# Grouped-query attention of a fused four-layer kernel: value and output weights folded into one product, heads summed in one PSUM bank, and the stage written out as a fixed order of pairs

## The chip, the cores and the metric

The kernel runs on one core of one Trainium2 chip. A core has TensorE (PE, with its weight loads listed apart as PEld), VectorE (DVE), ScalarE (ACT), GpSimd (POOL) and SyncE (SP, which here only issues transfers). The metric is the device time of one execution in microseconds (us). Before the change the median of three runs is 2576.98 us, from 2571.02 to 2581.21.

## The reference, cut to what matters

Four layers run one after another on `x` of shape (4, 512, 128): a gated scan, a mixture of eight experts, grouped-query attention, and six layers of windowed attention with a feed-forward. After each layer the input is added and a layer normalisation follows. The change lies in the third, with `NH, NKV, D = 8, 4, 128` and T = 512 positions a row:

```
q = (x @ Wq).reshape(b, t, NH, D).transpose(0, 2, 1, 3)
k = (x @ Wk).reshape(b, t, NKV, D).transpose(0, 2, 1, 3)
v = (x @ Wv).reshape(b, t, NKV, D).transpose(0, 2, 1, 3)
q = q * cos + rotate_half(q) * sin
k = k * cos + rotate_half(k) * sin
k, v = repeat(k, 2, axis=1), repeat(v, 2, axis=1)
attn = einsum('bhtd,bhsd->bhts', q, k) / sqrt(D)
attn = softmax(where(causal, -inf, attn))
out  = einsum('bhts,bhsd->bhtd', attn, v)
return out.transpose(0, 2, 1, 3).reshape(b, t, NH * D) @ Wo
```

Two query heads share one key and value head. The output is linear in `v` and in `Wo`, so `(attn @ v_kv) @ Wo_h` equals `attn @ (x @ (Wv_kv @ Wo_h))`, and the sum over the heads can be taken in any order.

## The kernel before, in words

Everything is float32 but the masks, which are bfloat16 and reach the scores through a product with a bfloat16 identity (`ident_h`). The 512 positions of a row are four chunks of 128. PSUM has eight banks of 512 float32 columns: the tags "mm" and "tr" have two one-bank buffers each that are used in turn, and "S" and "o" have one buffer of two banks each. The batch rows are `xB[b]` on entry to the third layer and `xA[b]` on leaving it.

The stage runs over 32 steps, one for each row b and query head h, and lets three pieces of work overlap by lag: at step i it projects head i, does the softmax of head i-1 and weighs the values of head i-2.

- `project`: with the first head of a row it transposes the row (`x2T`) and makes the values of all four key heads (L362, copied out to `V`). For each key head, and for each query head, `rotated` makes one 512-column product (L340), three products with the cosine and sine tables on DVE (L344, L346) and one sum on POOL (L350).
- `softmax`: for each of the four chunks of queries, of 128, 256, 384 and 512 keys, a mask product of the whole width (L387) and the score product (L390) add up in one bank of "S" or "o". DVE takes the maximum (L393) and scales it (L394), ACT takes the exponential and its sum (L397). When all four are done DVE takes the reciprocal (L401) and divides the four chunks (L404).
- `weigh`: ten 128 x 128 transposes (L419) in four groups, four copies to `gpT` (L423), four products of `V` with them that add up in one bank (L426), and a copy to `oT`. After the last head of a row, 32 products with `Wo` (L436) sum the heads, DVE adds the row (L441), and the layer normalisation follows.

The copies out of PSUM go through `evac`, which gives two of three to ACT (L86) and the third to DVE (L88), by a running count. Beyond the loops' lag, the order of the instructions on each engine is left to the tile framework's scheduler. The fourth layer, further on, is handled otherwise: its steps are a list written by hand (`TURN`), and manual dependencies keep every engine to that order.

Two things about the surroundings are used below. The stage's buffers take memory that the expert stage frees when its last row is normalised. The fourth layer starts when the last row of `xA` has been normalised, transposed and copied to `sA`; its first product is L550.

Of the kernel before, what the change touches and what calls it, by code (L numbers as in the profile page):

```python
# [8 lines left out]
F32 = mybir.dt.float32  # L9
BF16 = mybir.dt.bfloat16  # L10
AF = mybir.ActivationFunctionType
ALU = mybir.AluOpType
AX = mybir.AxisListType
PSUM = bass.MemoryType.PSUM

P = 128
B, T, D = 4, 512, 128
NC = T // P
# [8 lines left out]
NH, NKV = 8, 4  # L27
GSCALE = 128.0**-0.5
# [28 lines left out]
C_COS, C_SIN = 0, 512  # L57
# [10 lines left out]
def fused(ctx: ExitStack, tc: tile.TileContext, a: dict, out: bass.AP):  # L68
    nc = tc.nc

    cp = ctx.enter_context(tc.tile_pool(name="const", bufs=1))
    sm = ctx.enter_context(tc.tile_pool(name="small", bufs=4))
# [3 lines left out]
    def psum(tag, name):  # L76
        if tag in ("S", "o"):
            return pp.tile([P, 2, 512], F32, tag=tag, name=name, bufs=1)
        return pp.tile([P, 512], F32, tag=tag, name=name)
# [3 lines left out]
    def evac(o, i):  # L83
        turn[0] += 1
        if turn[0] % 3:
            nc.scalar.copy(o, i)  # L86
        else:
            nc.vector.tensor_copy(o, i)  # L88

    def chunks(x):  # L90
        return x.rearrange("p (c d) -> p c d", c=NC)
# [3 lines left out]
    cst = cp.tile([P, NCONST], F32, name="cst")  # L95
    ident = cp.tile([P, P], F32, name="ident")
# [12 lines left out]
    causal = mask_h[:, 2 * M_BAND :]  # L109
# [24 lines left out]
    def layernorm(o, i, tag):  # L134
        normalise(o, i, *statistics(i, tag))

    def transposed(i, tag):

        tp = psum("tr", f"tp_{tag}")
        for c in range(NC):  # L140
            nc.tensor.transpose(tp[:, c * P : (c + 1) * P], i[:, c, :], ident)  # L141
        return tp


    lwp = ctx.enter_context(tc.tile_pool(name="w_l", bufs=2))
    before_l = ctx.enter_context(ExitStack())
# [5 lines left out]
    with ExitStack() as stage:  # L152
# [28 lines left out]
        nc.sync.dma_start(gwq, a["gwq"])  # L181
        gwk = gwp.tile([P, NKV * D], F32, name="gwk")
        nc.sync.dma_start(gwk, a["gwk"])
        gwv = gwp.tile([P, NKV * D], F32, name="gwv")
        nc.sync.dma_start(gwv, a["gwv"])
        gwo = gwp.tile([P, NH, D], F32, name="gwo")
        nc.sync.dma_start(gwo, a["gwo"].rearrange("(h p) d -> p h d", p=P))

# [145 lines left out]
    with ExitStack() as stage:  # L334
        wk = stage.enter_context(tc.tile_pool(name="g", bufs=2))

        def rotated(w, xT, tag):

            q = psum("mm", f"rq_{tag}")
            nc.tensor.matmul(q, lhsT=w, rhs=xT, start=True, stop=True)  # L340
            t1 = wk.tile([P, T], F32, tag="t1", name=f"t1_{tag}")
            t2 = wk.tile([P, T], F32, tag="t2", name=f"t2_{tag}")
            o = wk.tile([P, T], F32, tag="rot", name=f"rot_{tag}", bufs=6)
            nc.vector.tensor_tensor(t1, q, cst[:, C_COS : C_COS + T], ALU.mult)  # L344
            for to, of in ((0, 64), (64, 0)):
                nc.vector.tensor_tensor(  # L346
                    t2[to : to + 64, :], q[of : of + 64, :],
                    cst[of : of + 64, C_SIN : C_SIN + T], ALU.mult,
                )
            nc.gpsimd.tensor_tensor(o, t1, t2, ALU.add)  # L350
            return o

        batch = {}

        def project(b, h):
            if h == 0:
                x2T = wk.tile([P, T], F32, tag="x2T", name=f"x2T{b}")
                evac(x2T, transposed(xB[b], f"x2_{b}"))
                V = wk.tile([P, NC, NKV * D], F32, tag="V", name=f"V{b}")
                for c in range(NC):  # L360
                    v = psum("mm", f"v{b}_{c}")
                    nc.tensor.matmul(  # L362
                        v, lhsT=x2T[:, c * P : (c + 1) * P], rhs=gwv, start=True, stop=True
                    )
                    evac(V[:, c, :], v)
                oT = wk.tile([P, NH, T], F32, tag="oT", name=f"oT{b}", bufs=1)
                batch[b] = {"x": x2T, "V": V, "o": oT}
            s = batch[b]
            kv = h // (NH // NKV)
            if h % (NH // NKV) == 0:  # L370
                s["k", kv] = rotated(gwk[:, kv * D : (kv + 1) * D], s["x"], f"k{b}_{kv}")
            s["q", h] = rotated(gwq[:, h * D : (h + 1) * D], s["x"], f"q{b}_{h}")

        def softmax(b, h):
            s = batch[b]
            qT, kT = s["q", h], s["k", h // (NH // NKV)]
            m = sm.tile([P, NC], F32, tag="m", name=f"gm{b}_{h}")
            nb = sm.tile([P, NC], F32, tag="nb", name=f"gnb{b}_{h}")
            su = sm.tile([P, NC], F32, tag="su", name=f"gsu{b}_{h}")
            pr = wk.tile([P, NC, T], F32, tag="gpr", name=f"gp{b}_{h}")  # L380
            for i2 in range(NC // 2):
                S = psum("So"[i2], f"gs{b}_{h}_{i2}")
                for i1 in range(2):
                    i = 2 * i2 + i1
                    n = (i + 1) * P
                    sc = S[:, i1, 0:n]
                    nc.tensor.matmul(  # L387
                        sc, lhsT=ident_h, rhs=causal[:, T - n :], start=True, stop=False
                    )
                    nc.tensor.matmul(  # L390
                        sc, lhsT=qT[:, i * P : n], rhs=kT[:, 0:n], start=False, stop=True
                    )
                    nc.vector.tensor_reduce(m[:, i : i + 1], sc, AX.X, ALU.max)  # L393
                    nc.vector.tensor_scalar(  # L394
                        nb[:, i : i + 1], m[:, i : i + 1], -GSCALE, None, ALU.mult
                    )
                    nc.scalar.activation(  # L397
                        pr[:, i, 0:n], sc, AF.Exp, bias=nb[:, i : i + 1], scale=GSCALE,
                        accum_out=su[:, i : i + 1],
                    )  # L400
            nc.vector.reciprocal(su, su)  # L401
            for i in range(NC):
                n = (i + 1) * P
                nc.vector.tensor_scalar(  # L404
                    pr[:, i, 0:n], pr[:, i, 0:n], su[:, i : i + 1], None, ALU.mult
                )
            s["p", h] = pr

        def weigh(b, h):
            s = batch[b]  # L410
            kv = h // (NH // NKV)
            pr = s["p", h]
            o = psum("mm", f"go{b}_{h}")
            pT = []
            for j in range(NC + 1):
                if j < NC:
                    pt = psum("tr", f"gpt{b}_{h}_{j}")
                    for i in range(j, NC):
                        nc.tensor.transpose(  # L419
                            pt[:, i * P : (i + 1) * P], pr[:, i, j * P : (j + 1) * P], ident  # L420
                        )
                    pT.append(wk.tile([P, T], F32, tag="pT", name=f"gpT{b}_{h}_{j}", bufs=4))
                    evac(pT[j][:, j * P :], pt[:, j * P :])  # L423
                if j:
                    k = j - 1
                    nc.tensor.matmul(  # L426
                        o[:, k * P :], lhsT=s["V"][:, k, kv * D : (kv + 1) * D],
                        rhs=pT[k][:, k * P :], start=k == 0, stop=k == NC - 1,
                    )
            evac(s["o"][:, h, :], o)  # L430
            if h < NH - 1:
                return
            y = psum("mm", f"gy{b}")
            for c in range(NC):
                for k in range(NH):
                    nc.tensor.matmul(  # L436
                        y[:, c * P : (c + 1) * P], lhsT=s["o"][:, k, c * P : (c + 1) * P],
                        rhs=gwo[:, k, :], start=k == 0, stop=k == NH - 1,
                    )
            r = wk.tile([P, NC, D], F32, tag="r", name=f"gr{b}")  # L440
            nc.vector.tensor_tensor(r, chunks(y), xB[b], ALU.add)  # L441
            layernorm(xA[b], r, f"g{b}")

        todo = [(b, h) for b in range(B) for h in range(NH)]
        for i in range(len(todo) + 2):
            if i < len(todo):
                project(*todo[i])
            if 1 <= i <= len(todo):
                softmax(*todo[i - 1])
            if i >= 2:  # L450
                weigh(*todo[i - 2])

    before_l.close()

# [1 line left out]
    with ExitStack() as stage:  # L456
# [398 lines left out]
        while steps:  # L855
            advance()

        order = mybir.DependencyInfo(mybir.DependencyClass.NoSync, mybir.DependencyReason.DATA)
        last = {}
        for ins in traced[first:]:  # L860
            if ins.engine in last:
                tc.add_manual_dep(ins, last[ins.engine].name, order, reason="the order written")
            last[ins.engine] = ins


def _constants(np):
# [40 lines left out]
def _layout(np, i):  # L907


    def per_feature(v):  # L910
# [28 lines left out]
        "eb2": i["L0_ffn_b2"],  # L939
        "gwq": i["L1_attn_Wq"],  # L940
        "gwk": i["L1_attn_Wk"],
        "gwv": i["L1_attn_Wv"],
        "gwo": i["L1_attn_Wo"],
        "lwqkv": i["L1_ffn_Wqkv"],
        "lwo": i["L1_ffn_Wo"],
# [23 lines left out]
```

## Time and profile before

| | us |
|---|---|
| median of three runs | 2576.98 |
| lowest, highest | 2571.02, 2581.21 |
| the profiled execution, device time | 2581.88 |
| the profiled execution, span of its instructions | 2580.1 |
| last product of the experts (L310) | at 342.5 |
| first product of the third layer on `x2T` (L362) | at 348.5 |
| last sum of the heads (L441) starts | at 734.4 |
| first product of the fourth layer (L550) | at 742.5 |

The span is counted from the first instruction to the last. TensorE's mean granted clock is 0.951 of full speed. Over the whole span PE is busy 87%, DVE 75%, POOL 54% and ACT 52%, but that is a mean over four layers with different limits: the third layer holds only the stretch from about 343 to 739 us.

A float32 matrix product is recorded as two passes, each with its own weight load, and a transpose as one. The duration of a pass counts from its start to its end, and the next pass starts well before that end, so what a product costs is read from the distance of starts, or from a row of many.

### The profile page before, as it was taken

How to read it: one execution, taken by the hardware profiler on the slowest of the kernel's cores; microseconds unless marked ns; L12 is line 12 of the kernel's file. 1: busy time of each engine (PE TensorE's matmuls, PEld its weight loads, DVE VectorE, ACT ScalarE, POOL GpSimd, SP SyncE). 2: the span in 40 equal slices, each digit the busy share in tenths (PEclk: the TensorE clock that was granted, in tenths of full speed). 3: DMA queues.
4: the chain of work that ended last, by engine and by line, in shares of the span. 5: the costliest groups of instructions: out<-in, count | busy, mean ns of one | idle time of the engine just before them, and what ended most of it. 6: DMA issues, size and time to landing. Idle time of an engine off the chain costs nothing.

```text
span 2580.1 us, 80423 instructions
## 1 busy us (share of the span) xinstructions
PE 2239.3 (87%) x33872; PEld 1485.8 (58%) x33968; DVE 1923.6 (75%) x4052; ACT 1333.5 (52%) x3203; POOL 1394.2 (54%) x1002
## 2 busy tenths in 40 slices
PE   3699988888879899989999999998999998989885
PEld 2466644554546566656666666665666665656552
DVE  6444456666759888888888888887888988888863
ACT  1111123233336566666676656666666666666542
POOL 2000011111148777776777777777677777777650
PEclk6699999999999999999999999999999999999997
DMA  6000000000002322232222312222222321212220
GB/s 197 1 1 1 1 1 1 1 1 1 1 7 75 93 60 58 66 92 59 56 66 54 106 51 66 52 71 84 59 60 66 93 66 51 65 50 67 56 55 24
DMA packets 85380, 131.11 MB, mean 51 GB/s; under 512 B 15894, under 2 KB 33564, under 8 KB 84124
## 3 DMA queue, kind: packets, MB, share of 16 engines
q1 hardware_dynamic: 82172, 122.87, 17.6%
q8 instruction: 268, 4.39, 0.7%
q10 hardware_dynamic: 2848, 3.10, 0.4%
q14 instruction: 92, 0.75, 0.1%
HBM read 25.82 MB, written 1.05 MB: 10 GB/s over the span
## 4 chain that ended last, share of the span: by engine, by line
PE 51%; DVE 10%; issue 6%; POOL 1%; ACT 1%; DMA 1%; SPq 0%; POOLq 0%; DVEq 0%; ACTq 0%
PE q L550 10%; PE ly L729 6%; PE lv L603 6%; PE tp_r L141 5%; PE lo L702 5%; PE ls L655 4%; PE tp_on L141 4%; PE fa L768 2%; PE lpt L689 2%; PE fy L778 2%; PE fg L757 2%; DVE lt L563 1%; DVE lt L567 1%; DVE on L713 1%; PE ls L643 1%
## 5 line engine op out<-in xcount | busy, mean ns | idle before, releaser
L572 POOL TENSOR_TENSOR ro<-lt,lt 128x512 f32<-128x512 f32 x384 | 483.5, 1269 | 158.3 <-DVE lt L567 130.0
L679 ACT ACTIVATE lp<-ls,lnb,rn 128x64 f32<-128x64 f32 x1536 | 482.4, 431 | 78.4 <-DVE lnb L670 77.9
L550 PE MATMUL q<-wqkv,sA 128*128 128x512 f32 x768 | 399.9, 603 | 2.8 <-ACT sq L555 1.5
L586 POOL TENSOR_TENSOR rk<-rk,neg_half 128x16 f32<-128x16 f32 x96 | 278.8, 2905 | 147.4 <-DVE rk L582 144.6
L586 POOL TENSOR_TENSOR rn<-rn,neg_half 128x16 f32<-128x16 f32 x96 | 278.9, 2905 | 146.9 <-DVE rn L582 138.5
L563 DVE TENSOR_TENSOR lt<-q,rot 128x512 f32<-128x512 f32 x384 | 262.5, 684 | 72.4 <-ACT sq L555 61.6
L607 ACT COPY vr<-lv 128x512 f32<-128x512 f32 x192 | 113.6, 592 | 388.6 <-PE lv L603 388.2
L555 ACT ACTIVATE sq<-q 128x512 f32<-128x512 f32 x384 | 235.1, 612 | 137.0 <-PE q L550 116.6
L141 PEld LDWEIGHTS tp_r<-ident,ro 128*128 128x128 f32 x1536 | 186.5, 142 | 164.8 <-issue 114.8
L567 DVE TENSOR_TENSOR lt<-q,rot 128x512 f32<-128x512 f32 x384 | 260.8, 679 | 0.0
L575 DVE TENSOR_REDUCE ss<-sq 128x8 f32<-128x512 f32 x384 | 259.6, 676 | 0.0
L702 PEld LDWEIGHTS lo<-vk,lpT 64*32 64x32 f32 x12288 | 143.3, 110 | 187.4 <-issue 153.8
L702 PE MATMUL lo<-vk,lpT 64*32 64x65 f32 x12288 | 183.5, 234 | 59.3 <-issue 36.3
L603 PE MATMUL lv<-wqkv,sA 128*128 128x512 f32 x384 | 220.9, 659 | 3.9 <-DVE lnb L670 2.2
L141 PE MATMUL tp_r<-ident,ro 128*128 128x128 f32 x1536 | 216.5, 274 | 8.9 <-POOL ro L572 7.6
L655 PE MATMUL ls<-kT,qT 64*32 64x64 f32 x12288 | 155.1, 226 | 72.6 <-issue 72.6
L593 POOL TENSOR_TENSOR ro<-ro,rk 128x512 f32<-128x512 f32 x192 | 196.1, 1042 | 7.5
L729 PE MATMUL ly<-oT,lwo 128*128 128x128 f32 x1536 | 188.9, 276 | 1.4 <-DVE lt L567 1.2
L729 PEld LDWEIGHTS ly<-oT,lwo 128*128 128x128 f32 x1536 | 182.2, 193 | 13.1 <-issue 10.6
L655 PEld LDWEIGHTS ls<-kT,qT 64*32 64x32 f32 x12288 | 134.1, 105 | 81.1 <-issue 80.2
L550 PEld LDWEIGHTS q<-wqkv,sA 128*128 128x128 f32 x768 | 127.3, 194 | 69.0 <-issue 49.4
L666 DVE TENSOR_REDUCE lm<-ls 128x16 f32<-128x1024 f32 x96 | 117.2, 1221 | 52.3 <-PE ls L655 51.4
(184 smaller groups left out, 3949.2 us busy)
## 6 DMA issues: line engine op xcount, KB each, us to landing
vk<-vr SPq DMA_DIRECT2D x576, 130.0 KB, 2.4
vk<-vr SPq DMA_DIRECT2D x336, 65.0 KB, 2.0
wqkv<-in_lwqkv_dram SPq DMA_DIRECT2D x6, 1536.0 KB, 7.0
ew<-in_ew_dram SPq DMA_DIRECT2D x16, 256.0 KB, 6.1
lwo<-in_lwo_dram SPq DMA_DIRECT2D x6, 512.0 KB, 8.8
lw<-in_lw_dram SPq DMA_DIRECT2D x6, 341.0 KB, 10.3
cst<-in_cst_dram ACTq DMA_DIRECT2D x1, 1028.0 KB
x_in<-in_x_dram ACTq DMA_DIRECT2D x4, 256.0 KB
```

The source lines that it names most:

```text
L141: nc.tensor.transpose(tp[:, c * P : (c + 1) * P], i[:, c, :], ident)
L550: nc.tensor.matmul(q, lhsT=self.xs, rhs=self.w["qkv"][:, j * 512 : (j + 1) * 512], start=True, stop=True,)
L563: nc.vector.tensor_tensor(heads(t1), heads(q), cs[:, None, :].to_broadcast([P, 8, DH]), ALU.mult)
L567: nc.vector.tensor_tensor(swapped(t2), swapped(q)[:, :, ::-1, :], sn[:, None].to_broadcast([P, 8, 2, 32]), ALU.mult,)
L572: nc.gpsimd.tensor_tensor(self.rot[j], t1, t2, ALU.add)
L575: nc.vector.tensor_reduce(self.ss[:, j * 8 : j * 8 + 8], heads(self.sq[j]), AX.X, ALU.add)
L586: nc.gpsimd.tensor_tensor(r, r, neg_half.to_broadcast([P, HEADS]), ALU.pow)
L603: nc.tensor.matmul(v, lhsT=self.xs, rhs=self.w["qkv"][:, (4 + j) * 512 : (5 + j) * 512], start=True, stop=True,)
L655: nc.tensor.matmul(S[to : to + QB, par, s, :], lhsT=self.qT[lo : lo + 64, s, to : to + QB], rhs=self.kT[lo : lo + 64, s, to : to + KB], st ...
L679: nc.scalar.activation(self.P[:, i, :], self.S[:, i % 2, i // 2 * KB : (i // 2 + 1) * KB], AF.Exp, bias=self.nb[:, i : i + 1], scale=self. ...
L702: nc.tensor.matmul(o[to : to + QB, par, i, :], lhsT=self.pT[lo : lo + KB, 4 * g + i, to : to + QB], rhs=vk[r][lo : lo + KB, 4 * g + i, :], ...
L729: nc.tensor.matmul(y, lhsT=self.w["o"][:, j, :], rhs=self.oT[:, j, :], start=j == 0, stop=j == INNER // P - 1,)
```

## The change

- **Weights.** `gwv` is loaded from a transposed copy as four blocks. Eight products make `wov`, one block for each query head, the product of its value and output weights.
- **Values.** `values` makes the values with `wov` for the two heads of a pair, so 256 columns for each chunk, in two banks and two copies on ACT. There is no `oT` and there are no products with `Wo` at the end: `weigh` has the transposed probabilities as the stationary operand and adds all heads of a row into one bank (`row.bank`), ten products of 128 columns for each head. Odd and even rows use the two banks of "o".
- **Masks.** Only the diagonal 128 x 128 block of each chunk gets a mask product. The keys before it are a product of their own, so the queries' chunk is loaded as weights twice.
- **Softmax.** The query tables are scaled once (`qtab`) and the maximum is negated where it is taken, so the scaling of the maximum falls away. The two heads of a pair use "S" (three chunks) and half a bank of "mm" (chunk 1).
- **Division** moves from DVE to POOL, as four products with a broadcast reciprocal. The reciprocal stays on DVE.
- **Transposes.** The ten blocks are packed as 4, 4 and 2 in three banks: the first and last group are copied by ACT, the middle one by DVE.
- **Order.** The work runs over 16 pairs (a row and a key head with its two query heads). `TURN` lists the 27 pieces of one turn with their lags, and `in_order` keeps every engine to the order in which they are written.

```diff
+        gwv = gwp.tile([P, NKV, D], F32, name="gwv")
+        nc.sync.dma_start(gwv, a["gwv"].rearrange("(h p) d -> p h d", p=P))
...
+        qtab = wk.tile([P, 2 * T], F32, name="qtab", bufs=1)
+        nc.vector.tensor_scalar(qtab, cst[:, C_COS : C_COS + 2 * T], GSCALE, None, ALU.mult)
...
+        for k in range(2):
+            p = psum("mm", f"wov{k}")
+            for i in range(4):
...
+                nc.tensor.matmul(
+                    p[:, i * D : (i + 1) * D], lhsT=gwv[:, kv, :], rhs=gwo[:, h, :],
+                    start=True, stop=True,
+                )
+            evac(wov[:, 4 * k : 4 * k + 4, :], chunks(p))
...
+            def begin(self):
+                if self.kv == 0:
+                    tp = transposed(xB[self.b], f"x2_{self.b}")
+                    self.row.x = wk.tile([P, T], F32, tag="x2T", name=f"x2T{self.b}")
+                    nc.scalar.copy(self.row.x, tp)
...
+            def values(self, k):
...
+                v = psum("mm", f"v{self.tag}_{k}")
+                for i in range(2):
+                    c = 2 * k + i
                     nc.tensor.matmul(
+                        v[:, i * 256 : (i + 1) * 256], lhsT=self.row.x[:, c * P : (c + 1) * P],
+                        rhs=wov[:, 2 * self.kv : 2 * self.kv + 2, :].rearrange("p h d -> p (h d)"),
+                        start=True, stop=True,
+                    )
+                nc.scalar.copy(
+                    self.V[:, 2 * k : 2 * k + 2].rearrange("p c h d -> p (c h d)"), v
+                )
...
+            def scores(self, t):
+
+                S = psum("S", f"gs{self.tag}_{t}")
+                mm = psum("mm", f"gs1{self.tag}_{t}")
+                self.S[t] = {3: S[:, 0], 2: S[:, 1, 0:384], 0: S[:, 1, 384:512], 1: mm[:, 0:256]}
+                for i, sc in self.S[t].items():
+                    n = i * P
+                    q = self.q[t][:, n : n + P]
+                    if i:
+                        nc.tensor.matmul(
+                            sc[:, 0:n], lhsT=q, rhs=self.k[:, 0:n], start=True, stop=True
+                        )
                     nc.tensor.matmul(
+                        sc[:, n:], lhsT=ident_h, rhs=causal[:, T - P :], start=True, stop=False
                     )
                     nc.tensor.matmul(
+                        sc[:, n:], lhsT=q, rhs=self.k[:, n : n + P], start=False, stop=True
+                    )
+
+            def maxes(self, t):
+
+                self.m[t] = m = sm.tile([P, NC], F32, tag="m", name=f"gm{self.tag}_{t}")
+                for i, sc in self.S[t].items():
+                    nc.vector.tensor_reduce(m[:, i : i + 1], sc, AX.X, ALU.max, negate=True)
+
+            def exps(self, t):
...
+                for i, sc in self.S[t].items():
                     nc.scalar.activation(
+                        self.pr[t][:, i, 0 : (i + 1) * P], sc, AF.Exp,
+                        bias=self.m[t][:, i : i + 1], scale=1.0, accum_out=su[:, i : i + 1],
+                    )
+
+            def divide(self, t):
+                r = self.su[t]
+                nc.vector.reciprocal(r, r)
+                for i in self.S[t]:
+                    p = self.pr[t][:, i, 0 : (i + 1) * P]
+                    nc.gpsimd.tensor_tensor(
+                        p, p, r[:, i : i + 1].to_broadcast([P, (i + 1) * P]), ALU.mult
+                    )
+
+
+            PARTS = (
+                ((0, 0), (1, 0), (2, 0), (3, 0)), ((1, 1), (2, 1), (3, 1), (3, 3)), ((2, 2), (3, 2)),
+            )
+
+            def flip(self, t, k, engine):
...
+                pt = psum("tr", f"gpt{self.tag}_{t}_{k}")
+                n = len(self.PARTS[k])
+                for s, (i, j) in enumerate(self.PARTS[k]):
+                    nc.tensor.transpose(
+                        pt[:, s * P : (s + 1) * P], self.pr[t][:, i, j * P : (j + 1) * P], ident
+                    )
...
+            def weigh(self, t, k):
...
+                for s, (i, j) in enumerate(self.PARTS[k]):
                     nc.tensor.matmul(
+                        y[:, i * P : (i + 1) * P], lhsT=self.pT[t][:, 4 * k + s, :],
+                        rhs=self.V[:, j, t, :], start=h == k == s == 0,
+                        stop=h == NH - 1 and k == 2 and s == 1,
+                    )
...
+        TURN = (
+            (0, "begin"), (1, "scores", 0), (1, "maxes", 0), (1, "exps", 0), (0, "key"),
+            (2, "flip", 1, 0, nc.scalar), (2, "flip", 1, 1, nc.vector),
+            (2, "flip", 1, 2, nc.scalar), (0, "query", 0), (2, "weigh", 1, 0),
+            (2, "weigh", 1, 1), (2, "weigh", 1, 2), (2, "finish"), (1, "divide", 0),
+            (0, "values", 0), (1, "scores", 1), (1, "maxes", 1), (1, "exps", 1), (0, "query", 1),
+            (1, "flip", 0, 0, nc.scalar), (1, "flip", 0, 1, nc.vector),
+            (1, "flip", 0, 2, nc.scalar), (0, "values", 1), (1, "weigh", 0, 0),
+            (1, "weigh", 0, 1), (1, "weigh", 0, 2), (1, "divide", 1),
+        )
...
+        for i in range(B * NKV + 2):
+            if i < B * NKV:
+                made.append(Pair(i, rows))
+            for lag, what, *of in TURN:
+                if 0 <= i - lag < B * NKV:
+                    getattr(made[i - lag], what)(*of)
+        in_order(traced[first:])
```

`key` and `query` call `rotated`, which is as before but for the tables it is given, and `finish` is the sum with the row and the layer normalisation, as before. The removed lines are those of the functions shown above. `in_order` is the loop of manual dependencies that stood at the end of the fourth layer, now a function that both layers call.

## The prediction

> **What bounds the kernel now.** I began with the windows, since the page's 87% for PE is a mean over four layers. One 100 us stretch lies in the experts, one in the third layer (columns: length, busy time of PE, PEld, DVE, ACT and POOL with counts, granted clock, transfers):
>
> ```profile
> 200.00:300.00 100.00, 100.00 (x557) 69.45 (x556) 40.38 (x111) 19.24 (x28) 2.01 (x2) 1.00 0.00 1
> ...
> 500.00:600.00 100.00, 83.77 (x360) 50.69 (x359) 67.43 (x178) 33.24 (x98) 16.17 (x13) 0.95 0.00 1
> ```
>
> In the third layer no engine is full, and even the clock has dropped. The groups of this layer (busy us, mean ns of one, idle time before and its cause) and its waits (us in total, times, longest) say who holds whom:
>
> ```profile
> L346 DVE TENSOR_TENSOR t_q<-rq_q,cst 64x512 f32<-64x512 f32 x64 | 44.0, 688 | 1.1
> L404 DVE TENSOR_SCALAR gp<-gp,gsu 128x512 f32<-128x512 f32 x32 | 15.3, 480 | 0.0
> L397 ACT ACTIVATE gp<-gs,gnb 128x512 f32<-128x512 f32 x32 | 22.0, 688 | 24.0 <-DVE gnb L394 23.6
> ```
>
> ```profile
> ACT gpT L86 <- PE gpt L419: 121.8, 59, 8.7
> ACT gp L397 <- DVE gnb L394: 92.6, 58, 8.8
> DVE gm L393 <- PE gs L390: 64.4, 49, 3.2
> PE gs L387 <- ACT gp L397: 13.5, 20, 1.8
> PE go L426 <- DVE gnb L394: 11.1, 6, 2.6
> ```
>
> ACT waits for DVE, DVE for PE, PE for both: a ring of hand-overs. A waiting PE also loses speed. PE's instructions around 509 us (start, duration, and in brackets the idle time before):
>
> ```profile
> 509.30 2.08 PE L426 MATMUL go<-gpT,V 128*128 128x512 f32 x2 [2.57 <-DVE gnb L394]
> ...
> 512.66 1.91 PE L390 MATMUL gs<-rot_k,rot_q 128*128 128x512 f32 x2
> ...
> 522.77 1.02 PE L390 MATMUL gs<-rot_k,rot_q 128*128 128x512 f32 x2
> ```
>
> The window of these 4 us has the clock, third from the end, at 0.50:
>
> ```profile
> 508.00:512.00 4.00, 2.70 (x5) 1.36 (x6) 1.31 (x5) 1.33 (x5) 1.21 (x1) 0.50 0.00 0
> ```
>
> After 2.57 us of idleness the same product takes twice as long, until 516. The chain that ended last has its pieces in the fourth layer alone, so it says nothing here.
>
> **PE's work.** In a row of many (44 passes in 5.08 us) a 128-column pass takes 0.112 us, so a float32 product of 128 columns 0.22; by distances of starts 256, 384 and 512 columns take 0.44, 0.65 and 0.86, a transpose 0.11, a 128-column mask 0.05. Before, each head has scores 0.22+0.44+0.65+0.86 = 2.17, masks 0.53, four switches between mask and score of about 0.06, query and half a key 1.29, transposes 1.1, values weighed 2.17, `Wo` 0.90, its share of `V` 0.43: 8.83 us, 283 for 32 heads, in a stretch of 391. After: scores 2.19, masks 0.21, switches 0.24, rotations 1.29, transposes 1.1, `weigh` 10 x 0.22 = 2.24, values 2 x 0.44 = 0.88: 8.15, or 261. PE's work shrinks by 22 us; the rest must come from less waiting.
>
> **One turn by hand.** Each engine keeps the written order. Let S0 start at 0, at full clock.
> - PE: S0 (first scores) to 2.65, key to 3.5, two transpose groups of head 1 to 4.4. The third needs the first one's "tr" bank.
> - DVE: maxima (0.69, 0.55, 0.29, 0.42) 1.05 to 3.15; key rotation, three of 0.69, to 5.7; copy (0.68) to 6.4. The vanished scalings (L394, 0.148 each) shorten each path to an exponential.
> - ACT: exponentials with their sums (0.78, 0.67, 0.46, 0.56) 1.8 to 4.3. Behind them is the copy of the first group: 4.9. So PE stands 0.55 and does the third group at 4.95, query 0 to 5.85, `weigh` to 8.1, `values` to 9.0, S1 to 11.65, query 1 to 12.6.
> - DVE rotates query 0 to 8.0 and takes the reciprocal, 8.2. POOL adds (1.27) to 9.3 and then divides.
> - Division's price D: the trace has no such row on POOL. L516, L511 and L572 (two tensors) give 0.46, 0.73 and 1.27 us for 128, 256 and 512; with about 1.0 for 384, D = 3.5. L593, a multiplication by a broadcast as here, takes 1.04 for 512; at that ratio D = 2.85. Proportional to columns from L593 it is 2.6; with the longest L516 and L511 (0.90 and 1.17) and 1.70 for 512 (L230), 5.2. I take 3.0, near L593, and keep 2.6 and 5.2. Division ends at 12.3, as PE arrives; query 1's sum, queued behind it on POOL, is due only in the next turn, and so is the second division.
> - Transposes of head 0 are held like those of head 1: exponentials end at 13.5, copy 14.1, third group 14.4 (0.55 lost again), `values` 15.3, `weigh` 17.5.
>
> A turn is 17.5 us: 16.3 of PE, 1.1 of stops. DVE has 11.6, ACT 8.2, POOL 3 x 1.27 + 2D = 9.8, all under cover. If PE gets faster, that cover is gone: ACT's copies behind the exponentials come next.
>
> **Gpsimd instead of VectorE.** L404 takes about 1.3 us for four, against D = 3.0. The Trainium skill, "GPSIMD Engine Reference", section Engine selection, advises VectorE for elementwise work and calls GpSimd about twice slower with two inputs; the rows here say 2.3 times. By the rule the division would stay on DVE and end near 9.5, but PE comes only at 12.6: the sum of an ordinary turn is the same. Only where the layer normalisation delays the reciprocal does it cost 1.7 us, three times, 5 us in all, contained below.
>
> **Clock.** The same skill, "TensorE: Matmul & The Clock Gate", section HAM oscillation, gives the rule of no idle gaps over about 3.4 us. By it stops of 0.55 leave the clock full and a turn 17.5. The trace shows half speed after 2.57 us already and a mean of 0.95. I take 0.97, 0.5 us a turn, and 0.4 for hand-overs that the walk rounds away: T = 18.4. By the rule alone the 14 full turns would be 7 us shorter.
>
> **The rest.**
> - `wov` (8 x 0.22) lies in PE's idle 343 to 348; its two copies and `qtab` (about 1 us of DVE) must wait for the experts' memory, as `x2T` did until 347.8. No cost beyond what turn 0 holds. The transposed `gwv` is the same one issue on SP, of the same size, with `gwo` behind it; the page shows the transfers quiet long before 343: nothing. Nothing else is queued on SP or POOL in this layer.
> - Turn 0 (no scores): copies, then four rotations and values through two "mm" banks that DVE frees every 2 us: 347.6 to 356.6. Turn 1: 16, to 372.6.
> - 14 turns x 18.4 = 257.6.
> - `finish` of rows 0 to 2: sum and normalisation take 734.4 to 738.8 = 4.4 us on DVE, with a POOL step (L125) inside. Reciprocal, division and next maxima stand behind it, then exponentials; PE stands some 3 us. With the slower clock after such a gap 5 a time, 15.
> - `begin` of rows 1 to 3: 3 x 0.5 = 1.5.
> - The two draining turns: 24.3 to the end of the last normalisation. The 32 `Wo` products that ended the stage (64 passes, 7.1 us) are gone.
>
> 347.6 + 9.0 + 16 + 257.6 + 15 + 1.5 + 24.3 = 671, against 738.8: 68 us. The fourth layer (1840 us) is untouched. Masks on PE, the merged copies on ACT and DVE and `oT` are worth nothing by themselves beyond the PE sum. The profiled execution took 2581.9, 4.9 above the median, so 2577 - 68 = **2509**.
>
> **Rivals.**
> 1. PE is filled (chance 0.13): hand-overs hide, T = 16.8, normalisations cost 2 each: 22 + 9 more, 2478. For it: the experts run at 100% and clock 1.00. Against: ACT's copies stand behind exponentials.
> 2. Half clock in every turn (0.14): one stretch as at 508 each, 2.5 us less 0.5 already counted, over 17 turns 34 us: 2543. For it: 0.50 there; against: my stops are a fifth of that gap.
> 3. Order isn't the limit (0.05): the written order replaces one set of waits by another, and only PE's work and the ended tail, 22 + 7, are gained: 2548.
> 4. GpSimd becomes the bound (0.06, slower). The division ends at 9.3 + D, and the first group's copy after it must precede PE's third group. Beyond D = 3.6 every us of D lengthens the turn by one. The 68 us are 4.25 for each of 16 turns, so from D = 7.9 the kernel is slower; at D = 10, 16 x 2.1 = 34 us, 2611. For it: POOL rows double under other work (L516: 0.46 to 0.90). Against: it takes more than twice the dearest estimate but 5.2, and that one costs only 1.6 a turn, 26 us.
>
> **How the numbers follow.** The likeliest case has 0.62; with D at 5.2 or the clock lower it reaches 2540, with the clock full 2490. From 2472 to 2548 it is joined by rivals 1 and 2 and half of 3; outside is under 0.15. About 0.5%, 13 us, is what a measurement of this kernel can tell from no change. Only rival 4 and mixtures of 2 and 3 come near: faster 0.91, same 0.03, slower 0.06.
>
> **What would show it.** Right: L550 starts near 675; PE busy over 90% in this layer; turns near 18.4; division's four rows sum to 2.6 to 3.5; PE's short waits are for ACT copies of `gpT` and, in three turns, for POOL. Wrong: clock under 0.9, D over 5, POOL near 90% busy, or PE waiting mainly for the division.

## The result, and the profile after

The changed kernel takes 2534.18 us (median of four runs, 2532.6 to 2540.57) against 2578.06 for the kernel before. The ratio of the means is 0.9838, with a 95% interval from 0.9811 to 0.9865. That is 44 us faster, where 68 were forecast. The profiled execution took 2532.6, with a span of 2530.5.

Not all of the 44 belongs to the third layer. The fourth layer's first product (L550 before, L636 after) moved from 742.5 to 705.4: 37.1 us. The other 12.5 us between the two spans (2580.1 - 2530.5 = 49.6) lie in the fourth layer, whose code is the same. From its start to the end it took 1837.6 us before, 1825.1 after, and in the experiments' profiles between 1823 and 1843. So below some 10 us the total says little, and the start of the fourth layer is the sharper measure. It is used from here on, beside the ratios. Even it moves by some 3 us with the start of the stage: the first score product comes at 354.8 in the kernel after and between 355.6 and 358.2 in its variants below. Each ratio is against the kernel before on the same chip, where it took 2570 to 2586.

The windows of the kernel after, for the same two stretches as before:

```profile
200.00:300.00 100.00, 100.00 (x557) 69.45 (x556) 41.09 (x110) 19.24 (x28) 2.01 (x2) 1.00 0.00 1
500.00:600.00 100.00, 81.39 (x529) 65.55 (x529) 54.03 (x110) 33.95 (x103) 43.20 (x52) 0.98 0.00 1
```

PE still stands a fifth of the third layer; POOL has gone from 16 to 43 of 100 us and is not full; the clock is 0.98. The groups of this layer after the change, 343 to 705:

```profile
L468 POOL TENSOR_TENSOR gp<-gp,gsu 128x512 f32<-128x512 f32 (+3 forms) x128 | 88.0, 719 | 16.7 <-DVE gsu L465 16.7
...
L503 PE MATMUL gy<-V,gpT 128*128 128x128 f32 x640 | 81.2, 285 | 2.7 <-ACT gpT L487 2.7
...
L452 DVE TENSOR_REDUCE gm<-gs 128x1 f32<-128x512 f32 (+3 forms) x128 | 53.8, 483 | 124.4 <-PE gs L444 124.4
...
L483 PE MATMUL gpt<-ident,gp 128*128 128x128 f32 x320 | 50.1, 287 | 60.8 <-ACT gpT L487 49.2 <-POOL gp L468 9.6 <-DVE gpT L487 1.9
```

The 32 divisions, of four instructions each, take 88.0 / 32 = 2.75 us on POOL. PE's idle time before the transposes (L483), 60.8 us, is most of what it stands in this layer. The waits say how it is cut up (us in total, times, longest):

```profile
DVE gm L452 <- PE gs L444: 124.4, 29, 6.9
...
ACT gp L458 <- PE rq_k L405: 71.6, 15, 6.5
...
PE gpt L483 <- ACT gpT L487: 49.2, 28, 1.9
...
PE gpt L483 <- POOL gp L468: 9.6, 6, 2.9
```

These are the two waits that the prediction named, ACT's copies and the division beside the normalisations. But the first is 1.9 us long at worst and comes 28 times, so nearly every stop is at its longest; 0.55 was forecast. One half turn shows where that comes from. In this timeline (start, duration, engine and line, idle time before in brackets), the first scores S0 start at 482.46:

```profile
482.46 0.81 PE L438 MATMUL gs<-rot_k,rot_q 128*128 128x384 f32 x2
...
483.16 0.44 PE L444 MATMUL gs<-rot_k,rot_q 128*128 128x128 f32 x2
...
484.26 0.44 PE L444 MATMUL gs<-rot_k,rot_q 128*128 128x128 f32 x2
...
484.74 1.68 DVE L452 TENSOR_REDUCE gm<-gs 128x1 f32<-128x512 f32 x4 [5.30 <-PE gs L444]
...
485.95 1.04 PE L483 MATMUL gpt<-ident,gp 128*128 128x128 f32 x8
486.21 0.69 ACT L458 ACTIVATE gp<-gs,gm 128x512 f32<-128x512 f32 x1 [5.20 <-PE rq_k L405]
...
488.14 0.21 ACT L458 ACTIVATION_READ_ACCUMULATOR gp<-gs,gm 128x1 f32 x1
488.23 0.60 ACT L487 COPY gpT<-gpt 128x512 f32<-128x512 f32 x1
...
488.88 0.44 PE L483 MATMUL gpt<-ident,gp 128*128 128x128 f32 x2 [1.89 <-ACT gpT L487]
```

Chunk 3 is complete with the product of 483.16. Its maximum does not start then, but at 484.74, after the product of chunk 0 at 484.26: 2.28 us after S0 began, not 1.05. Its exponential does not follow the first maximum's end, 0.69 later, but starts at 486.21, when about three of the four maxima are done. So ACT's copy comes at 488.23, 5.77 after S0, and PE stands 1.89 us. The second half of the turn has the same stop. An ordinary turn, from one first score product S0 to the next, with no `begin` and no normalisation in it, is 20.45 us, against 18.4 forecast and 17.5 walked.

A profile names releasers by the clock. "PE rq_k L405" is the key projection, which the exponential does not read; it happens to end at about that time. In the program as built, these waits are kept for a PSUM tile as a whole, not for the part that is read or written. Chunks 3, 2 and 0 share the two-bank tile "S". The maximum of chunk 3 waits there for the count that the product of chunk 0 brings, and the first exponential for the count that the maximum of chunk 0 brings.

### The profile page after: what moved, and what is told of

Same layout as the page of the kernel before. It is cut to its first block, busy times and chain, and to the rows that moved or that the text cites. A ratio compares the mean times of both kernels' runs of the same rounds, so it can differ in the third digit from the quotient of the medians.

```text
span 2530.5 us, 81144 instructions
## 1 busy us (share of the span) xinstructions
PE 2193.2 (87%) x34400; PEld 1511.5 (60%) x34400; DVE 1854.9 (73%) x3769; ACT 1322.6 (52%) x3185; POOL 1480.9 (59%) x1130
## 3 DMA queue, kind: packets, MB, share of 16 engines
q1 hardware_dynamic: 82556, 122.87, 18.4%
HBM read 25.82 MB, written 1.05 MB: 11 GB/s over the span
## 4 chain that ended last, share of the span: by engine, by line
PE 55%; DVE 8%; issue 6%; ACT 1%; DMA 1%; POOL 1%; SPq 0%; POOLq 0%; DVEq 0%; ACTq 0%
PE q L636 11%; PE lv L689 7%; PE ly L815 6%; PE tp_r L141 6%; PE lo L788 5%; PE ls L741 4%; PE tp_on L141 4%; PE lpt L775 3%; PE fa L854 2%; PE fy L864 2%; PE fg L843 2%; PE ls L729 1%; DVE lt L649 1%; DVE lt L653 1%; DVE on L799 1%
## 5 line engine op out<-in xcount | busy, mean ns | idle before, releaser
L636 PE MATMUL q<-wqkv,sA 128*128 128x512 f32 x768 | 395.3, 597 | 3.6 <-ACT sq L641 2.2
L788 PE MATMUL lo<-vk,lpT 64*32 64x65 f32 x12288 | 180.4, 230 | 46.9 <-issue 26.5
L636 PEld LDWEIGHTS q<-wqkv,sA 128*128 128x128 f32 x768 | 126.2, 192 | 66.6 <-issue 43.3
```

The costliest lines, as they stand in the source:

```text
L636: nc.tensor.matmul(q, lhsT=self.xs, rhs=self.w["qkv"][:, j * 512 : (j + 1) * 512], start=True, stop=True,)
L788: nc.tensor.matmul(o[to : to + QB, par, i, :], lhsT=self.pT[lo : lo + KB, 4 * g + i, to : to + QB], rhs=vk[r][lo : lo + KB, 4 * g + i, :], ...
```

## Experiments

**1. Is it the shared tile?** Chunk 3 gets a one-bank tile of its own, chunks 2 and 0 share another. As before they take two banks, and the products and the order stay. (The edit also gives each layer's score tiles a pool of their own, so that the other layers keep their two-bank tile.)

```diff
-                S = psum("S", f"gs{self.tag}_{t}")
+                s3 = psum("S3", f"gs3{self.tag}_{t}")
+                s2 = psum("S2", f"gs2{self.tag}_{t}")
...
-                self.S[t] = {3: S[:, 0], 2: S[:, 1, 0:384], 0: S[:, 1, 384:512], 1: mm[:, 0:256]}
+                self.S[t] = {3: s3, 2: s2[:, 0:384], 0: s2[:, 384:512], 1: mm[:, 0:256]}
```

> The only change to the changed kernel: the two-bank score tile S becomes two tiles of one bank, chunk 3 in its own, chunks 2 and 0 in the other. Order on every engine, instructions and banks stay. Theory A (the maximum of chunk 3 waits for the product of chunk 0, and the exponential of chunk 3 for the maximum of chunk 0, because they share one PSUM tile and waits are kept by tile): maxima of a head begin 1.2 us after its first score product instead of 2.3, exponentials end at 4.8 instead of 5.9, PE's two stops of 1.89 a turn shrink to about 0.85, an ordinary turn is 18.4 instead of 20.45 us, the kernel 2502 us. Rival B (the exponentials really wait for PE, the key or query product after the scores): nothing moves, turn 20.45, 2534 us. Rival C (ACT's own work is too slow): stop stays near 1.9.

Measured: 2504.37 us, ratio 0.969 (0.964 to 0.9739); the fourth layer starts at 666.5, 38.9 us earlier than after the change. The timeline of the same half turn, S0 at 468.06:

```profile
468.06 0.81 PE L451 MATMUL gs<-rot_k,rot_q 128*128 128x384 f32 x2
...
469.24 0.69 DVE L465 TENSOR_REDUCE gm<-gs 128x1 f32<-128x512 f32 x1 [3.02 <-PE gs L457]
...
470.03 0.69 ACT L471 ACTIVATE gp<-gs,gm 128x512 f32<-128x512 f32 x1 [3.41 <-DVE gm L465]
...
472.55 0.59 ACT L500 COPY gpT<-gpt 128x512 f32<-128x512 f32 x1
...
473.20 0.44 PE L496 MATMUL gpt<-ident,gp 128*128 128x128 f32 x2 [0.60 <-ACT gpT L500]
```

The first maximum starts 1.18 after S0, the first exponential 1.97, ACT's copy 4.49; the stop is 0.60 and the turn 17.88. The first four are within 0.2 us of the walk in the prediction (1.05, 1.8, 4.3, 0.55), and the turn is 0.4 above its 17.5. The walk was right for this kernel and not for the one that it was made for. The exponential's releaser is now named as the maximum, and the key projection is gone from that place.

A second kernel also takes chunk 0 out of the tile of chunk 2:

```diff
-                self.S[t] = {3: s3, 2: s2[:, 0:384], 0: s2[:, 384:512], 1: mm[:, 0:256]}
+                self.S[t] = {3: s3, 2: s2[:, 0:384], 0: mm[:, 256:384], 1: mm[:, 0:256]}
```

> As e1_split, but chunk 2 has a one-bank tile of its own too, and chunk 0 moves into the mm bank of chunk 1. Theory A: exponentials end at 4.55 us after the first score product, stops about 0.6, turn 17.8, kernel 2494 us. Rival B: 2534 us. If only the first link of the chain matters, as e1_split.

Measured: 2499.54 us, ratio 0.9667 (0.9611 to 0.9723); fourth layer at 663.5, turn 17.59, stop 0.46. Most of the gain was in chunk 3.

**2. Does the division on GpSimd cost anything?** It goes back to DVE:

```diff
-                    nc.gpsimd.tensor_tensor(
-                        p, p, r[:, i : i + 1].to_broadcast([P, (i + 1) * P]), ALU.mult
-                    )
+                    nc.vector.tensor_scalar(p, p, r[:, i : i + 1], None, ALU.mult)
```

> The changed kernel with the division back on DVE (four multiplications of 0.3 to 0.5 us, as before), all else the same. Theory of the prediction: the division is hidden in an ordinary turn on either engine, so it stays at 20.45 us; in the three turns with a layer normalisation it is 1.5 us shorter, 2530 us in all. Rival (DVE's queue is what the move relieves): the maxima behind it start later, the turn grows by up to 2.6 us, 2570 us.

Measured: 2545.72 us, ratio 0.9843 (0.9795 to 0.9892), by the interval not told apart from the kernel after; fourth layer at 711.2, 5.8 us later than after the change. An ordinary turn is 20.41, as with GpSimd (20.45). The three turns with a normalisation are 25.99, 26.5 and 25.2, where GpSimd has 24.62, 23.92 and 23.76: 5.4 us in all. (The stage also began 2.5 us later, and a turn with a clock dip of 1.6 that the kernel after has is missing here.) One of these turns, with the division on DVE:

```profile
453.14 1.28 DVE L468 TENSOR_SCALAR gp<-gp,gsu 128x512 f32<-128x512 f32 x4
...
454.33 1.68 DVE L452 TENSOR_REDUCE gm<-gs 128x1 f32<-128x512 f32 x4
...
458.45 0.69 PE L481 MATMUL gpt<-ident,gp 128*128 128x128 f32 x2 [2.99 <-ACT gpT L485]
```

And with GpSimd, in the kernel after:

```profile
452.25 1.66 DVE L452 TENSOR_REDUCE gm<-gs 128x1 f32<-128x512 f32 x4
452.41 2.75 POOL L468 TENSOR_TENSOR gp<-gp,gsu 128x512 f32<-128x512 f32 x4 [1.32 <-DVE gsu L465]
...
454.65 2.89 PE L483 MATMUL gpt<-ident,gp 128*128 128x128 f32 x10 [2.94 <-POOL gp L468]
```

On DVE the division (1.28 us) stands ahead of the late maxima, which everything else waits for. On POOL it takes 2.75, but beside them. Counted from the S0 of their turn, these maxima start 16.14 us in with DVE and 14.86 with POOL, later by just the 1.28.

**3. Can the normalisation be hidden in the written order?** `finish` moves behind the last transposes of the turn, where DVE has slack:

```diff
-            (2, "weigh", 1, 1), (2, "weigh", 1, 2), (2, "finish"), (1, "divide", 0),
+            (2, "weigh", 1, 1), (2, "weigh", 1, 2), (1, "divide", 0),
...
-            (1, "flip", 0, 2, nc.scalar), (0, "values", 1), (1, "weigh", 0, 0),
+            (1, "flip", 0, 2, nc.scalar), (2, "finish"), (0, "values", 1), (1, "weigh", 0, 0),
```

> The changed kernel with the sum and layer normalisation of a finished row moved from ahead of the first division to behind the last copy of the turn's transposes. Theory: the three turns that take 23.8 to 24.6 us come down to about 21.2 (the second reciprocal is now behind it, and the next turn's first transposes wait some 0.8 us for POOL), 2526 us. Rival: the delay only moves into the next turn through the second division, sum of the two turns unchanged, 2534 us.

Measured: 2537.63 us, ratio 0.9816 (0.9767 to 0.9866), which cannot be told from the kernel after. The turns with a normalisation fell to 20.45, so the 11 us are hidden. The fourth layer starts at 700.0, only 5.4 us earlier. The stage began 2.2 us later, and three other turns of this execution took about 1.65 us more, where the kernel after has one such turn. There the clock had dropped (the section on the hardware has such a place).

**4. What does the written order itself give?** The call of `in_order` is left out for the third layer; everything else stays, and the scheduler chooses.

```diff
-        in_order(traced[first:])
```

> The changed kernel without the manual dependencies of its third layer: the same instructions, the order on each engine left to the scheduler. Theory (the written order is what removes most of the waiting, PE's work alone is worth about 22 us): the fourth layer starts near 715 instead of 705 and before's 742, 2550 us. Rival 3 of the prediction (the order isn't the limit): 2534 us, the same as with the order.

Measured: 2492.98 us, ratio 0.9709 (0.9666 to 0.9753); fourth layer at 664.7. This refutes the expectation: without the written order the stage is 40.7 us shorter. PE's instructions of a half turn with the scheduler's order:

```profile
489.86 1.04 PE L483 MATMUL gpt<-ident,gp 128*128 128x128 f32 x8
491.86 0.91 PE L438 MATMUL gs<-rot_k,rot_q 128*128 128x384 f32 x2 [0.96 <-ACT gp L458]
492.61 1.02 PE L405 MATMUL rq_q<-x2T,gwq 128*128 128x512 f32 x2
493.47 0.38 PE L483 MATMUL gpt<-ident,gp 128*128 128x128 f32 x2
```

After two groups of transposes the scheduler does not go on to the third, which waits for a copy. It puts in the next head's first score product and the query projection, and the third group finds its bank free. The stop is 0.96 instead of 1.89. In a turn with a normalisation the scheduler also sets a maximum between the steps of the normalisation. Such a turn takes 20.12 us and the one behind it 17.58, together only 0.3 more than two ordinary turns of 18.7.

The opposite edit gives the kernel before a written order, its own program order, by the same manual dependencies:

```diff
+        stage_ins = nc.cur_bb.bb.instructions
+        stage_first = len(stage_ins)
...
+        for ins in stage_ins[stage_first:]:
+            if ins.engine in last:
+                tc.add_manual_dep(ins, last[ins.engine].name, order, reason="the order written")
+            last[ins.engine] = ins
```

> The kernel before with one addition: every engine is kept to the order in which its third layer is written (project, softmax, weigh). Nothing else of the change. Theory N (the gain lies in the list of pairs, not in fixing an order): the same or slower than before, 2578 to 2620 us, with PE waiting between the four chunks of one head. Theory O (any fixed order beats the scheduler's): 2555 us.

Measured: 2801.94 us, ratio 1.0917 (1.0876 to 1.0957); fourth layer at 980.2. The loss is far larger than expected. Its waits from 357 to 950:

```profile
ACT gp L397 <- DVE gnb L394: 341.8, 125, 18.2
...
PE gs L387 <- ACT gp L397: 167.3, 62, 7.8
```

PE now stands 62 times before a mask product for an exponential to free its bank, with all its other work queued behind. In the scheduler's order of before these were 20 waits of 13.5 us in all.

**5. Which part of the scheduler's order matters?** In the written order of the kernel after, the two pieces that the scheduler had moved are moved by hand: the next head's first score product and the query projection go ahead of the third transposes. (`first` is that product, taken out of `scores`.)

```diff
-            (2, "flip", 1, 2, nc.scalar), (0, "query", 0), (2, "weigh", 1, 0),
+            (1, "first", 1), (0, "query", 0), (2, "flip", 1, 2, nc.scalar), (2, "weigh", 1, 0),
...
-            (1, "flip", 0, 2, nc.scalar), (0, "values", 1), (1, "weigh", 0, 0),
+            (0, "first", 0), (1, "flip", 0, 2, nc.scalar), (0, "values", 1), (1, "weigh", 0, 0),
```

> The changed kernel, order written, with two pieces of PE's order moved as the scheduler has them in e5_free: the first score product of the next head (384 columns, chunk 3) and the query product of the pair stand ahead of the third group of transposes, not behind it. Theory (the written order costs 41 us because PE's queue holds independent products behind transposes that wait for ACT's copy): ordinary turn 18.7 instead of 20.45, the fourth layer starts near 677, 2506 us. Rival (the scheduler gains elsewhere, on ACT's or DVE's order): turn stays near 20.4, 2534 us.

Measured: 2528.4 us, ratio 0.9816 (0.9784 to 0.9848); fourth layer at 690.1, 15.3 us earlier than after the change. The turn is 18.92. The waits from 357 to 640 have the new stop:

```profile
PE gs L434 <- ACT gp L467: 18.8, 23, 1.0
```

It is 1.0 at most, as in the scheduler's order. The 677 expected for the fourth layer was missed, and the rest of the 40.7 was not won: a turn with a normalisation and the one behind it together still cost 4.0 to 5.6 us more than two ordinary ones.

**6. How does the division do in the scheduler's order?** `in_order` is left out and the division is on DVE (both edits above).

> e5_free with the division back on DVE. Theory: as with the written order, an ordinary turn hides it on either engine (18.7 us) and the turns with a normalisation pay 2 us each, 2499 us. Rival (freed from the written order, PE is tight enough for DVE's 2.6 us a turn to count): turn 19.5 or more, 2510 us.

Measured: 2505.66 us, ratio 0.9717 (0.9677 to 0.9758); fourth layer at 671.4, against 664.7 with GpSimd. The ordinary turn is 18.66, no longer than the 18.7 with GpSimd. So the engine is of no account in an ordinary turn, whoever orders it. A turn with a normalisation and the one behind it together take 0.9 more than with GpSimd, 2.6 for the three, two clock dips of 1.6 aside; these dips and the stage's start and end make the rest of the 6.7.

**7. What do the narrow masks bring?** The full-width mask and score products come back; nothing else changes.

```diff
-                    if i:
-                        nc.tensor.matmul(
-                            sc[:, 0:n], lhsT=q, rhs=self.k[:, 0:n], start=True, stop=True
-                        )
...
-                        sc[:, n:], lhsT=ident_h, rhs=causal[:, T - P :], start=True, stop=False
+                        sc, lhsT=ident_h, rhs=causal[:, T - w :], start=True, stop=False
...
-                        sc[:, n:], lhsT=q, rhs=self.k[:, n : n + P], start=False, stop=True
+                    nc.tensor.matmul(sc, lhsT=q, rhs=self.k[:, 0:w], start=False, stop=True)
```

> The changed kernel with masks of the whole width again: one mask product and one score product for each chunk, as before. Theory: PE's score part is 0.27 us longer for a head (0.53 against 0.21 us of masks, less three fewer small products), and since the exponentials and both stops follow the scores it is not hidden: ordinary turn 21.0 instead of 20.45, 2543 us. Rival: it is hidden in the stops, 2534 us.

Measured: 2542.17 us over six runs, ratio 0.99 (0.9865 to 0.9935); fourth layer at 713.1. The ordinary turn is 20.68, so the narrow masks bring 0.23 a turn, 3.2 us over 14. Most of the other 4.5 us are two more turns with a clock dip (1.7 to 1.9 us each) in this execution.

**8. Put together.** Own tiles for the chunks and the late `finish`, in the written order:

> e2_own and e4_late_finish together. Theory: ordinary turns stay at 17.6 us, the three turns with a layer normalisation come from 22.0 to about 18.8 (the second division is late by 1.2 us for the next turn's transposes), the fourth layer starts near 654 instead of 663.5, 2490 us. Rival: at this shorter turn the late second division costs as much as it saves, 2500 us.

Measured: 2480.03 us, ratio 0.9656 (0.9621 to 0.969); fourth layer at 656.1, turn 17.6. The late `finish` is not quite hidden here: the turn with it takes 18.8 and the next 18.64. The same with the two pieces of part 5 moved:

> e8_own_late with the same two pieces moved, order written. Theory: PE's stops vanish, turn 17.0, 2473 us, as e9_free_own_late by hand. Rival: the moved product now waits for the exponentials of the head before it and makes a new stop of its own, turn 17.6 or more, 2480 us or above.

Measured: 2485.17 us, ratio 0.9643 (0.9608 to 0.9678); fourth layer at 645.6. An ordinary turn is 16.9, but the one behind each late `finish` is 18.91, which the theory did not have. And the own tiles and late `finish` without `in_order`:

> e8_own_late without the manual dependencies of the third layer. Theory (the scheduler pulls independent products of PE into its stops, as in e5_free; there is only some 0.46 us a stop left to fill): ordinary turn 17.0 instead of 17.6, the fourth layer starts near 647, 2473 us. Rival: with stops this short the written order costs nothing any more, 2480 us.

Measured: 2476.21 us, ratio 0.9614 (0.9576 to 0.9651); fourth layer at 637.7, turn 17.0. A window of its third layer:

```profile
500.00:600.00 100.00, 99.44 (x649) 78.60 (x649) 72.90 (x151) 44.02 (x129) 56.84 (x68) 1.00 0.00 1
```

PE is full and at full clock: this is about the stage's limit with these products. By the median and by the layer's start it is the best of all the kernels, 67.7 us ahead of the kernel after in this stage. By their intervals the ratios of these three are not told apart.

## Why the prediction was right, and where it was not

**The bound, the direction and most terms were right.** Hand-overs bound the stage, and once they are gone PE does. PE's work in a turn was walked as 16.3 us; 20.45 - 2 x 1.89 = 16.67 were measured, and 17.0 is the turn of the kernel in which PE is full. The other terms of the walk came out near too. Turn 1 ended at 373.99 (372.6 forecast). The turns with a normalisation cost 4.17, 3.47 and 3.31 more (5 each), those with `begin` 0.43 more (0.5). The last normalisation came 28 us after the last full turn (24.3).

**Where the gain came from was not forecast, and that the total lies in the range is in part luck.** The prediction put 22 us down to PE's work and said that "the rest must come from less waiting". From 343 us to the first product of the fourth layer, before, after and with the scheduler's order of part 4 (the first two figures are the length and PE's busy time):

```profile
343.00:742.50 399.50, 322.53 (x1375) 192.57 (x1374) 262.65 (x702) 128.81 (x379) 65.71 (x53) 0.95 0.00 1
343.00:705.40 362.40, 286.02 (x1793) 227.40 (x1792) 194.50 (x412) 119.77 (x361) 152.78 (x181) 0.96 0.00 1
343.00:664.70 321.70, 278.32 (x1797) 222.43 (x1796) 193.55 (x417) 119.04 (x360) 152.33 (x181) 0.98 0.00 1
```

PE's busy time fell by 36.5 us. Its idle time was 77.0 us before and is 76.4 after: one set of waits took the place of another, as rival 3 has it, and the gain is PE's shorter busy time alone, more than the 22 and the ended tail. What the rest of the 36.5 is was not split; stretches at half clock are in it. The measured 2534 is 14 us from rival 3's 2548, which had a chance of 0.05, and 25 from 2509. The waiting shrinks only in the variants: to 43.4 us of idle time with the scheduler's order, 40.5 with the tile split, 15.0 in the last kernel of part 8.

**The step that failed is "maxima 1.05 to 3.15, exponentials 1.8 to 4.3, copy 4.9".** Measured, the maxima start at 2.28, the exponentials run from 3.75 to 5.9, and the stop is 1.89 instead of 0.55. The walk let each chunk go as soon as its own product was done; the shared tile does not. T became 20.45 instead of 18.4, and 14 x 2.05 = 28.7 us, nearly all of the 30 us by which the fourth layer missed 675 (705.4). The other misses nearly cancel: the normalisations and `begin` took 4.2 us less than put down, a clock dip, turn 1 and the end 5.9 more. With the tile split the same walk holds, and the layer starts at 666.5. So the mechanism of the stop, exponentials ahead of ACT's copy, was right, and its size was wrong. With it went "PE busy over 90%": it was 81%.

**Rival 3 was priced at the wrong end.** It had the written order as neutral at worst. The runs show a cost of 40.7 us: with the scheduler's order the same products and engines give 742.5 - 664.7 = 77.8 us, and the written order takes back over half. Of the 40.7, the ordinary turns make 14 x (20.45 - 18.7) = 24.5, the turns with a normalisation 10.95 less about 0.9, so 10, one clock dip 1.6; the rest, some 4.6, lies nearly all ahead of the full turns, whose first S0 comes at 369.6 instead of 374.0. What was gained came from the other parts of the change. How much each of those brought alone was tested only for the masks (3.2) and the division. Of the 77.8 us, 44.2 are PE's busy time and 33.6 its idle time. So in the scheduler's order something did shorten the ring: the removed scalings, the pairing or the merged copies, which the prediction had as worth nothing by themselves. Which of them did is open. The shared tile and the order overlap, since both act through the same stop: own tiles with the late `finish` leave 656.1 - 637.7 = 18.4 us between the two orders, and 7.9 with the two pieces moved too.

**GpSimd's division.** D was 3.0, measured 2.75; rival 4 needed 7.9. That an ordinary turn hides it on either engine held in both orders. "Only where the layer normalisation delays the reciprocal does it cost 1.7 us" had the wrong sign: in those turns DVE costs 1.4 to 2.6 us more. The advice of the Trainium skill ("GPSIMD Engine Reference", Engine selection), VectorE for elementwise work, is right on the duration: the division is 2.75 / 1.28 = 2.1 times as long on POOL. Here the queue decides, not the duration: on DVE the late maxima stand behind it.

**Rival 1 and rival 2.** PE was not filled by this kernel, though it can be (17.0). Half clock in every turn did not come; the mean granted clock from 357 to 690 was 0.97. The stretch at 508 before the change, on which rival 2 rests, ended at 514.7 by the clock's own record, not at 516.

## What to carry to other kernels

When you walk a schedule by hand, ask of each wait not what data the instruction needs but which tile it names: two banks in one PSUM tile are one thing to wait for, and giving the first consumer its own tile cost nothing here and saved 38.9 us. Write an engine order by hand only after a run with the scheduler's; where it loses, look at what the scheduler puts into the stops. An operation that is twice as slow on another engine can be the better choice when what matters is what queues behind it. And when a total comes out near, look whether the term that was to bring it did: here the waiting was to go, and the busy time went.

## What the runs showed of the hardware

Half speed came after shorter stops than the one of 2.57 us that the prediction shows. PE's instructions of the kernel after around 432, and three windows there:

```profile
432.39 0.44 PE L483 MATMUL gpt<-ident,gp 128*128 128x128 f32 x2 [1.89 <-ACT gpT L487]
...
433.76 3.79 PE L503 MATMUL gy<-V,gpT 128*128 128x128 f32 x20
```

```profile
434.00:437.00 3.00, 3.00 (x17) 3.00 (x17) 0.00 (x0) 0.59 (x1) 1.99 (x4) 0.55 0.00 0
429.86:433.27 3.41, 1.52 (x11) 1.24 (x10) 2.82 (x6) 2.85 (x10) 1.26 (x2) 1.00 0.00 0
433.27:436.69 3.42, 3.42 (x16) 3.28 (x16) 0.00 (x0) 0.59 (x1) 2.71 (x5) 0.50 0.02 5
```

The 20 passes take 3.79 us, and 2.39 in a turn at full clock; the turn is 1.63 longer. The stop was 1.89 us, below the 2.57 of the kernel before. Yet the same stop comes 28 times and mostly leaves the clock at 1.00: one ordinary turn with such a dip was seen in the kernel after, three in the one with the late `finish`. No ordinary turn of the split tile's kernel, with stops of 0.60, is longer by such an amount.

The clock's records in the traces narrow down what decides. Every stretch at half clock in this stage lasts 3.41 us or a multiple of it, and all those of one execution begin on one grid of that step; one of them is 433.27 to 436.69. In all 14 traces together, take the windows of this grid that are themselves at full clock, from 355 us to 640 (to 735 in the kernel before, to 960 in its ordered form). Where PE stood idle for more than 57.5% of the window, the next one was at half clock, in 61 of 61 cases. Where it stood less than 43%, in none of 998. Between the two it was in 17 of 107. A stop of 0.60 us is 18% of a window. One of 1.89 that lies whole in a window is 55%, inside the band: after 429.86 to 433.27 the clock dropped, after 603.90 to 607.32, with the same stop, it did not. What decides inside the band no run here shows. The rule of idle gaps that the prediction cites would have let all of these stops pass; the measurement decides.
